# Graph convolution with a sparse adjacency: tiled rounds merged with full products, the row tiles' turns given by ScalarE, loads and stores both on SyncE

## The chip, the cores and the metric

The kernel runs on one NeuronCore of one Trainium2 chip. The metric is the device time of one execution in microseconds (us); lower is better. Times before are nine runs of the unchanged kernel. The profile is one further execution, taken by the hardware profiler.

## The reference

One layer: a symmetrised, rectified adjacency matrix is normalised by its degrees, applied to features, and the result goes through a rectifier, a residual sum and a layer norm.

```python
HW = jnp.einsum('bnf,fo->bno', H, W)              # H = x: (8, 4096, 256), W: (256, 256)
A_norm = jax.nn.relu((A + A.T) * 0.5)             # A = adj: (4096, 4096), sparse
D = jnp.sum(A_norm, axis=1)
DAD = d_inv_sqrt[:, None] * A_norm * d_inv_sqrt[None, :]
out = jnp.einsum('nm,bmo->bno', jnp.eye(N) - DAD, HW)
x = _layernorm(x + jax.nn.relu(out), axis=-1)     # eps 1e-5
```

Low-numbered nodes have many edges, high-numbered ones few. All arithmetic of the products is float32.

## The kernel before, in words

**First half (to about 593 us).** The adjacency is read in 512x512 blocks, symmetrised, and written to DRAM as `a_dram`; the features are multiplied by W, scaled, and written as `g_dram` (4096 rows of 2048 floats: 8 batches x 256). Row block 0 of the result is accumulated along the way. The change does not touch this half, save that line numbers move.

**Second half (from about 593 us).** The remaining 31 blocks of 128 result rows are worked off in 16 *units* (`SEQ`), two row blocks a unit, called b0 and b1. A block's result is 128 x 2048 floats, four PSUM banks of 128 x 512 (`py`, tags b0 and b1, four banks each: all eight banks). For each unit only those rows of `g_dram` that matter are fetched: lists made on VectorE (with a few small matmuls, `lists`) say which source rows have edges into the unit. GpSimd gathers 128 such rows at a time into one of twelve ring buffers `g` (1 MB) and the matching pieces of `a_dram` into `ga`, each with an indirect DMA. 268 such gathers are made. A slot is filled again when the oldest tile in the ring has been used up (`gather_ahead`, called once after every step). Two further sets of 128 rows, the hubs, stay in SBUF; only their adjacency rows `gh` are loaded per block.

**Steps.** `steps_of(u)` makes the order of a unit. There are two sorts of step.

- A *full step* is one tile (hub or ring) against one block: four products of 128x128 weights by 512 columns, one into each bank.
- A *tiled step* (a round) has up to eight operations, each with 64 source rows and 32 result rows, so that up to eight sit side by side in TensorE's array as tiles of 64x32. `tiled` runs the round in four *turns*; in turn m the operations on the upper 64 source rows write bank m, those on the lower 64 write bank m+2 (mod 4). Two row tiles must not write the same bank at one time, so each turn waits for the turn before the last: a `nop` on SyncE (a *tick*, line 1194) waits for the last matmul of the turn, and the first matmul of the turn after next waits for the tick.

Every float32 matmul stands twice in the trace, as two passes. A full product is two records of 128x512, a turn of eight operations is sixteen records.

Before, a full step and a round are always separate steps: 114 full steps and 112 rounds (838 operations), so 456 full products and 448 turns.

**Around the steps.** `run_later(2)` runs once after each step and counts down deferred work. When the last product of a block is in, `finish` queues four evictions on ScalarE (`evict`, line 760: PSUM to `y`, one buffer only, so the next block's eviction waits for VectorE's sum of the block before, line 770), and one step later the sum `z + y`, the statistics (779) and the normalisation (803) on VectorE; 14 counts (`LATE`) after that comes the store on SyncE's queue (813). When b0 of a unit is finished, `lists` puts 36 small matmuls on TensorE one step later, into two of the four b0 banks just evicted; VectorE reads them (236 to 241, 443 to 459) before it does the sum of b0. The next unit's first product for b0 into those banks waits for these reads. The residual rows `xr` (1 MB each) are loaded on ScalarE's DMA queue (`residuals`, line 754), 6 and 10 counts into a unit. All instructions of one engine run in the order in which they were recorded; `queue(...)` pins them there.

Of the kernel before, what the change touches and what calls it, by code (L numbers as in the profile page):

```python
# [25 lines left out]
HUBS = [*[2] * 15, 0]  # L26
# [41 lines left out]
def kernel(  # L68
# [25 lines left out]
    nc = tc.nc  # L94
    B, N, F = x.shape
    FO = w.shape[1]
    P = 128
# [9 lines left out]
    QU = P // E  # L107
# [1 line left out]
    HOLD = 10  # L109
    RING = 12  # L110
    REACH = 5
    LATE = 14
    EPS = 1e-5
    NK = len(KINDS)
    L = 64
    mid = KINDS.index(16), KINDS.index(51)
# [354 lines left out]
    with (  # L471
# [71 lines left out]
        held = {}  # L543
# [208 lines left out]
    def residual(i, engine):  # L752
        xr = blocks_pool.tile([P, B, F], F32, tag="adj", name=f"xr_{i}")
        engine.dma_start(xr, x[:, i * P : (i + 1) * P, :].rearrange("b p f -> p b f"))
        return xr
# [63 lines left out]
    def steps_of(u):  # L819

        kind_at = {}
        for k, kind in enumerate(KINDS):
            for s in range(FIRST[u][k], FIRST[u][k] + CAPS[u][k]):
                kind_at[s] = kind
        every = 255 if blocks(u) == 2 else 15
        whole = {0: [], 15: [], 240: []}
        todo = []
        for t in range(tiles[u]):
            pair = kind_at.get(2 * t), kind_at.get(2 * t + 1)
            if pair[0] == pair[1] and pair[0] in whole:  # L830
# [24 lines left out]
        def full(t, b):  # L855
            return [(t, None, b, None)]

        def weave(*several):
            several = [list(s) for s in several]
            total = [len(s) for s in several]  # L860
            out = []
            while any(several):
                at = max(range(len(several)), key=lambda k: (len(several[k]) / max(total[k], 1), total[k]))
                out.append(several[at].pop(0))
            return out

        held = range(HUBS[u])
        out = [full(-1, 0)] if HUBS[u] else []
        starts = [full(t, 0) for t in whole[15]]
        if not out and starts:  # L870
            out.append(starts.pop(0))
        out += weave(rounds[:first_b1], [full(-1 - h, 0) for h in held[1:]], starts)
        if blocks(u) == 1:
            return out + [full(t, 0) for t in whole[0]]
        out += [full(-1, 1)] if HUBS[u] else []
        rows = [[full(t, 0), full(t, 1)] for t in whole[0]]
        between = [[r] for r in rounds[first_b1 : max(last_b0 + 1, first_b1)]]
        out += chain.from_iterable(weave(between, rows))
        out += weave(
            [full(-1 - h, 1) for h in held[1:]],  # L880
            [full(t, 1) for t in whole[240]],
            rounds[max(last_b0 + 1, first_b1) :],
        )
        return out

    with (
        tc.tile_pool(name="ypool", bufs=2) as ypool,
# [32 lines left out]
        def queue(engine):  # L920

            traced = reversed(nc.cur_bb.bb.instructions)
            return tc.issue_after(next(i for i in traced if i.engine == engines[engine]))
# [154 lines left out]

        def residuals(rows):
            for i in rows:  # L1080
                with queue("act"):
                    xr[i] = residual(i, nc.scalar)


        ahead = {u: {k: SEQ[n + k] for k in (2, 3, 4) if n + k < NU} for n, u in enumerate(SEQ)}
# [59 lines left out]
        def follow(this, other):  # L1145
            tc.add_manual_dep(
                this.ins,
                other.ins.name,
                mybir.DependencyInfo(mybir.DependencyClass.Sync, mybir.DependencyReason.DATA),
                reason="two row tiles of the array take turns at a bank",  # L1150
            )
# [16 lines left out]
        NC = G // S  # L1168


        def tiled(u, step, last):

            for m in range(NC):
                ins = None
                for i in range(2):
                    c = (m + 2 * i) % NC
                    for op in step:
                        if op[1] != i:
                            continue
                        before = ins  # L1180
                        ins = product(
                            u,
                            op,
                            c,
                            slice(i * L, (i + 1) * L),
                            slice(op[3] * E, (op[3] + 1) * E),
                            False,
                            op in last and m >= NC // 2,
                        )
                        if before is None:  # L1190
                            if len(ticks) > 1:
                                follow(ins, ticks[-2])
                with queue("sp"):
                    ticks.append(nc.sync.nop())
                follow(ticks[-1], ins)

        for q, (u, step) in enumerate(steps):
            new = q == 0 or steps[q - 1][0] != u
# [14 lines left out]
            for b in touched:  # L1213
                if not py[2 * u + 1 + b]:
                    py[2 * u + 1 + b] = [
                        psum.tile([P, S], F32, tag=f"b{b}", name=f"py_{u}_{b}_{c}") for c in range(NC)
                    ]
            if step[0][1] is None:
                (op,) = step
                b = op[2]  # L1220
                hs = {(b, e) for e in range(QU)}
                assert not hs & begun or hs <= begun
                for h in hs:
                    left[h] -= 1
                for c in range(NC):
                    product(
                        u, op, c, slice(0, P), slice(0, P), not hs & begun, not any(left[h] for h in hs)
                    )
                begun |= hs
            else:  # L1230
                for op in step:
                    assert op[2:] in begun
                    left[op[2:]] -= 1
                last = [op for op in step if not left[op[2:]]]
                tiled(u, step, last)
            for op in step:
                t = op[0]
                uses_left[u, t] -= 1
                if t < 0:
                    load_hub_rows(SEQ[SEQ.index(u) + 1 :], -1 - t, op[2])  # L1240
            gather_ahead()
            run_later(2)
            for b in touched:
                if not any(left[b, e] for e in range(QU)):
                    if b == 0:
# [67 lines left out]
```

## Time and profile before

| | us |
|---|---|
| median of 9 runs (lowest to highest) | 1511.09 (1510.16 to 1513.78) |
| the profiled execution, own time | 1517.72 |
| its span, first to last instruction | 1515.5 |
| first and last start of a `py` matmul (the second half) | 592.6 and 1498.6 |
| PE, DVE, ACT, POOL busy over the span | 1393.5, 1039.9, 364.5, 770.4 |
| mean granted TensorE clock | 0.964 |
| DMA, whole run | 543.04 MB, 358 GB/s |

On the page, PE is matmul, PEld weight loads, DVE VectorE, ACT ScalarE, POOL GpSimd, SP SyncE; a q behind a name is the engine's sequencer. Matmul ends are modelled (a 512-column pass reads 589 ns although the next one may start 429 ns after it), so a busy PE is not a PE at its peak. For the second half the starts of matmuls tell more than the busy share. Line 1159 is the matmul of all products, 1194 the tick, 944 and 952 the gathers.

### The profile page before, as it was taken

How to read it: one execution, taken by the hardware profiler on the slowest of the kernel's cores; microseconds unless marked ns; L12 is line 12 of the kernel's file. 1: busy time of each engine (PE TensorE's matmuls, PEld its weight loads, DVE VectorE, ACT ScalarE, POOL GpSimd, SP SyncE). 2: the span in 40 equal slices, each digit the busy share in tenths (PEclk: the TensorE clock that was granted, in tenths of full speed). 3: DMA queues.
4: the chain of work that ended last, by engine and by line, in shares of the span. 5: the costliest groups of instructions: out<-in, count | busy, mean ns of one | idle time of the engine just before them, and what ended most of it. 6: DMA issues, size and time to landing. Idle time of an engine off the chain costs nothing.

```text
span 1515.5 us, 29693 instructions
## 1 busy us (share of the span) xinstructions
PE 1393.5 (92%) x11008; PEld 755.9 (50%) x11008; DVE 1039.9 (69%) x3173; ACT 364.5 (24%) x462; POOL 770.4 (51%) x1564
## 2 busy tenths in 40 slices
PE   6999998989999987999999999999999899998984
PEld 5877877767777753333433433333333343433331
DVE  5676578979956463208595897797408988899644
ACT  3555554544445450000001001001000110011111
POOL 3444010011313314764766667767745777786762
PEclk9999999989999999899999999999999999999996
DMA  9999999999989997998999999999977999999995
GB/s 357 368 361 400 394 378 362 354 338 352 350 316 348 336 397 283 368 398 321 391 367 371 357 391 383 384 373 373 398 268 264 381 354 406 386 372 402 380 378 173
DMA packets 217160, 543.04 MB, mean 358 GB/s; under 512 B 19370, under 2 KB 109194, under 8 KB 182426
## 3 DMA queue, kind: packets, MB, share of 16 engines
q0 software_dynamic: 55664, 283.87, 48.5%
q1 hardware_dynamic: 93472, 126.89, 24.5%
q10 hardware_dynamic: 67872, 130.32, 23.0%
q8 instruction: 89, 1.46, 0.4%
q14 instruction: 63, 0.51, 0.1%
HBM read 438.03 MB, written 136.34 MB: 379 GB/s over the span
## 4 chain that ended last, share of the span: by engine, by line
PE 47%; DMA 23%; DVE 19%; issue 5%; POOL 3%; ACT 2%; ACTq 0%; SPq 0%; POOLq 0%; DVEq 0%
PE py L1159 27%; DMA g<-g_dram,gi 10%; PE pg L607 9%; DMA ga<-a_dram,ai 6%; PE lead L565 5%; DVE sym L500 4%; DMA a_dram<-sym 3%; DVE sums L507 3%; PE tr L496 3%; PE xtr L596 3%; DMA xin<-in_x_dram 2%; DVE stats L779 2%; DVE xr L770 1%; DMA adj<-in_adj_dram 1%; POOL g L952 1%
## 5 line engine op out<-in xcount | busy, mean ns | idle before, releaser
L1159 PE MATMUL py<-g,ga 64*32 64x512 f32 (+1 forms) x7136 | 625.8, 615 | 35.8 <-DMA g<-g_dram,gi 30.4
L1159 PEld LDWEIGHTS py<-g,ga 64*32 64x32 f32 (+1 forms) x7136 | 230.1, 114 | 415.2 <-issue 342.8
L944 POOL DMA_INDIRECT ga<-a_dram,ai x268 | 289.7, 1081 | 136.2 <-PE py L1159 63.4
L952 POOL DMA_INDIRECT g<-g_dram,gi x268 | 300.2, 1120 | 110.5 <-issue 62.2
L760 ACT ACTIVATE y<-py,minus_r 128x512 f32<-128x512 f32 x120 | 75.9, 688 | 801.6 <-PE py L1159 622.4
L607 PE MATMUL pg<-w_sb,xt 128*128 128x256 f32 x1024 | 229.7, 382 | 5.8 <-ACT xt L597 4.0
L1159 PE MATMUL py<-g_hub,gh 128*128 128x512 f32 x480 | 222.2, 605 | 3.7 <-DVE pos_k L240 3.7
L500 DVE TENSOR_TENSOR sym<-tr,adj 128x512 f32<-128x512 f32 x256 | 161.8, 680 | 80.8 <-PE tr L496 79.2
L607 PEld LDWEIGHTS pg<-w_sb,xt 128*128 128x128 f32 x1024 | 194.1, 192 | 33.6 <-ACT xt L597 4.4
L508 POOL TENSOR_SCALAR uses<-sums 128x64 uint8<-128x64 f32 x64 | 27.6, 431 | 311.4 <-DVE sums L507 262.3
L507 DVE TENSOR_REDUCE sums<-sym 128x64 f32<-128x2048 f32 x64 | 145.3, 2276 | 52.2 <-ACT sym L504 52.2
L496 PE MATMUL tr<-ident,adj 128*128 128x128 f32 x1024 | 139.6, 287 | 28.2 <-DVE sym L500 16.0
L1159 PEld LDWEIGHTS py<-g_hub,gh 128*128 128x128 f32 x480 | 88.1, 191 | 132.4 <-issue 119.5
L504 ACT ACTIVATE sym<-sym 128x2048 f32<-128x2048 f32 x64 | 122.8, 1918 | 126.2 <-DVE sym L500 126.2
L443 DVE TENSOR_SCALAR low<-lists 128x17 f32<-128x17 f32 (+8 forms) x14 | 2.5, 175 | 213.7 <-PE lists L431 213.7
L496 PEld LDWEIGHTS tr<-ident,adj 128*128 128x128 f32 x1024 | 119.5, 147 | 55.1 <-DVE sym L500 33.5
L770 DVE TENSOR_TENSOR xr<-xr,y 128x2048 f32<-128x2048 f32 x31 | 70.8, 2285 | 50.9 <-ACT y L760 44.9
L596 PE MATMUL xtr<-ident,xin 128*128 128x128 f32 x512 | 74.1, 294 | 15.3 <-DVE sym L500 14.5
L803 DVE TENSOR_SCALAR xr<-xr,mv,root 128x256 f32<-128x256 f32 x248 | 84.6, 411 | 1.1
L779 DVE BATCH_NORM_STATS2 stats<-xr 128x6 f32<-128x256 f32 x248 | 84.1, 412 | 1.1
L565 PE MATMUL lead<-gt,strip 128*128 128x512 f32 x176 | 82.6, 593 | 0.0
L597 ACT COPY xt<-xtr 128x512 f32<-128x512 f32 x128 | 68.0, 592 | 45.9 <-PE xtr L596 36.9
(157 smaller groups left out, 1057.7 us busy)
## 6 DMA issues: line engine op xcount, KB each, us to landing
adj<-in_adj_dram SPq DMA_DIRECT2D x64, 1024.0 KB, 11.0
a_dram<-sym ACTq DMA_DIRECT2D x64, 1024.0 KB, 9.7
out_dram<-xr SPq DMA_DIRECT2D x31, 1024.0 KB, 20.3
xr<-in_x_dram ACTq DMA_DIRECT2D x28, 1024.0 KB, 20.6
xin<-in_x_dram SPq DMA_DIRECT2D x44, 512.0 KB, 11.7
g_dram<-gt ACTq DMA_DIRECT2D x22, 1024.0 KB, 7.6
xin<-in_x_dram POOLq DMA_DIRECT2D x20, 512.0 KB
g_dram<-held ACTq DMA_DIRECT2D x10, 1024.0 KB, 12.0
```

The lines of the kernel that those rows point to most:

```text
L496: ins = nc.tensor.transpose(pt[:, c * P : (c + 1) * P], tji[:, c, a * P : (a + 1) * P], ident)
L500: nc.vector.tensor_add(sym[:, a, :], pt, tij[:, a, :])
L504: nc.scalar.activation(sym, sym, AF.Relu, scale=0.5)
L507: nc.vector.tensor_reduce(sums, sym.rearrange("p a (c q) -> p a c q", q=E), AX.X, ALU.add)
L565: nc.tensor.matmul(lead[c], lhsT=strip, rhs=g[:, c * S : (c + 1) * S], start=not done, stop=len(done) == NB - 1, skip_group_check=True,)
L596: nc.tensor.transpose(pt[:, k, c, :], xin[b // H][:, b % H + k, c * P : (c + 1) * P], ident)
L607: ins = nc.tensor.matmul(pg[:, k * FO : (k + 1) * FO], lhsT=xt[:, b + k, c, :], rhs=w_sb[:, c, :], start=(c == 0), stop=(c == FC - 1),)
L770: nc.vector.tensor_add(z, z, y)
L779: nc.vector.bn_stats(stats[:, b, :], z[:, b, :])
L944: nc.gpsimd.indirect_dma_start(out=at if both else at[:, : E if one else P], out_offset=None, in_=a_pairs if both else a_groups if one els ...
L952: nc.gpsimd.indirect_dma_start(out=gt, out_offset=None, in_=g_dram, in_offset=bass.IndirectOffsetOnAxis(ap=gi[:, t : t + 1], axis=0), boun ...
L1159: return nc.tensor.matmul(py[2 * u + 1 + b][c][cols, :], lhsT=at[ps, off + cols.start : off + cols.stop], rhs=gt[ps, c * S : (c + 1) * S], ...
```

## The change

Rounds and full steps are merged. `beside` spreads the full steps of a stretch over its rounds; a round that gets one carries it as a ninth operation, and `tiled` puts one product of it behind every turn (bank m+1). The order within a unit is made anew: hub and early b0 products beside the rounds that touch only b0, everything in both blocks beside the middle rounds, and one full step (or the late rounds) at the end. Of 226 steps 157 are left: 45 full steps, 43 rounds without a full product, 69 rounds with one. Products and turns are the same in number (456 and 448). `run_later(2)` runs twice after a merged step.

The ticks move from SyncE to ScalarE (448 of them), the 28 residual loads from ScalarE's queue to SyncE's, where the stores are. `LATE` goes from 14 counts to 4.

```diff
-    LATE = 14
+    LATE = 4
...
+        def beside(several, fulls):
+
+            out, put = [], 0
+            for k, step in enumerate(several):
+                upto = len(fulls) * (k + 1) // len(several)
+                out.append(step + fulls[put] if put < upto else step)
+                out += fulls[put + 1 : upto]
+                put = max(upto, put)
+            return out + fulls[put:]
+
         held = range(HUBS[u])
-        out = [full(-1, 0)] if HUBS[u] else []
-        starts = [full(t, 0) for t in whole[15]]
-        if not out and starts:
-            out.append(starts.pop(0))
-        out += weave(rounds[:first_b1], [full(-1 - h, 0) for h in held[1:]], starts)
+        firsts = [full(-1 - h, 0) for h in held] + [full(t, 0) for t in whole[15]]
         if blocks(u) == 1:
-            return out + [full(t, 0) for t in whole[0]]
-        out += [full(-1, 1)] if HUBS[u] else []
-        rows = [[full(t, 0), full(t, 1)] for t in whole[0]]
-        between = [[r] for r in rounds[first_b1 : max(last_b0 + 1, first_b1)]]
-        out += chain.from_iterable(weave(between, rows))
-        out += weave(
-            [full(-1 - h, 1) for h in held[1:]],
-            [full(t, 1) for t in whole[240]],
-            rounds[max(last_b0 + 1, first_b1) :],
-        )
-        return out
+            return firsts[:1] + beside(rounds, firsts[1:]) + [full(t, 0) for t in whole[0]]
+        seconds = [full(-1 - h, 1) for h in held] + [full(t, 1) for t in whole[240]]
+        both = [full(t, b) for t in whole[0] for b in range(2)]
+        early, late = rounds[:first_b1], rounds[last_b0 + 1 :]
+        between = rounds[first_b1 : last_b0 + 1]
+        fills = firsts[1:] + both
+        ahead = min(len(firsts) - 1, len(early)) if between else len(firsts) - 1
+        kept = 0 if late else 1
+        mid = fills[ahead:] + (seconds[1 : len(seconds) - kept] if between else [])
+        rest = seconds[len(seconds) - kept :] if between else seconds[1:]
+        if late:
+            mid, rest = (fills[ahead:], seconds[1:])
+        return firsts[:1] + beside(early, fills[:ahead]) + seconds[:1] + beside(between, mid) + beside(late, rest)
...
         def residuals(rows):
             for i in rows:
-                with queue("act"):
-                    xr[i] = residual(i, nc.scalar)
+                with queue("sp"):
+                    xr[i] = residual(i, nc.sync)
...
-        def tiled(u, step, last):
+        def tiled(u, step, last, whole):
...
-                with queue("sp"):
-                    ticks.append(nc.sync.nop())
+                with queue("act"):
+                    ticks.append(nc.scalar.nop())
                 follow(ticks[-1], ins)
+                for op in whole:
+                    product(u, op, (m + 1) % NC, slice(0, P), slice(0, P), False, op in last)
...
+            alone = [op for op in step if op[1] is None]
+            if len(alone) == len(step):
...
             else:
...
+                assert all(hs <= begun for _, hs in spans)
+                tiled(u, [op for op in step if op[1] is not None], last, alone)
...
             gather_ahead()
-            run_later(2)
+            for _ in range(2 if 0 < len(alone) < len(step) else 1):
+                run_later(2)
```

The order at the end of a unit (F a full step, T8 a round of eight, T8F a round with a full product, 0 or 1 the block, ! where b0 is complete, * where b1 is). Unit 4 before: `F0 T8 F0 F0 F1 T6 F0 F1 T8 T8 T8 T8 T7! F1 F1*`; after: `F0 T8F0 F1 T6 T8F0 T8F0 T8 T8F1 T7F1! F1*`.

More of the change, by code (lines that the diff above doesn't have):

```diff
@@ L1217 @@
                     ]
[L1218 to L1222, printed above, removed]
+            spans = [(op, {tuple(op[2:])} if op[1] is not None else {(op[2], e) for e in range(QU)}) for op in step]
+            for _, hs in spans:
                 for h in hs:
                     left[h] -= 1
+            last = [op for op, hs in spans if not any(left[h] for h in hs)]
+            alone = [op for op in step if op[1] is None]
+            if len(alone) == len(step):
+                ((op, hs),) = spans
+                assert not hs & begun or hs <= begun
                 for c in range(NC):
-                    product(
-                        u, op, c, slice(0, P), slice(0, P), not hs & begun, not any(left[h] for h in hs)
-                    )
+                    product(u, op, c, slice(0, P), slice(0, P), not hs & begun, op in last)
                 begun |= hs
             else:
[L1231 to L1235, printed above, removed]
+                assert all(hs <= begun for _, hs in spans)
+                tiled(u, [op for op in step if op[1] is not None], last, alone)
             for op in step:
```

## The prediction

> **What bounds the kernel now.** Only the second half changes. It runs from 592.6 to 1498.6 us (906.0 us); before it and behind it the work is the same. I read the stretches first: busy time, granted clock, DMA share and rate.
>
> ```profile
> core 0: us, PE busy (x) PEld busy (x) DVE busy (x) ACT busy (x) POOL busy (x), PEclk, DMA share, GB/s
> 592.60:627.04 34.44, 24.09 (x130) 7.42 (x128) 19.92 (x61) 0.70 (x2) 27.14 (x26) 0.80 0.95 349
> ...
> 700.00:800.00 100.00, 100.00 (x908) 38.61 (x914) 76.57 (x287) 4.84 (x8) 69.39 (x65) 1.00 0.99 364
> ...
> 1100.00:1200.00 100.00, 95.47 (x1012) 35.65 (x1010) 56.41 (x213) 10.01 (x16) 60.05 (x60) 0.97 0.81 293
> ...
> 1300.00:1400.00 100.00, 90.22 (x920) 37.12 (x919) 92.50 (x345) 10.02 (x16) 76.69 (x72) 0.95 1.02 388
> ```
>
> TensorE is busy all through 700 to 800 at full clock: there nothing but its own pace counts. Later DMA is close behind (share 1.02 at 388 GB/s), and a gather comes late now and then. The waits say how much, over the second half (us in total, times, longest):
>
> ```profile
> ACT y L760 <- DVE xr L770: 151.6, 14, 14.9
> ...
> PEld py L1159 <- SPq L1194: 58.5, 203, 1.8
> ...
> PE py L1159 <- DMA g<-g_dram,gi: 30.4, 14, 5.8
> ...
> PE lists L294 <- DVE kind L284: 6.8, 2, 4.5
> ...
> PE lists L431 <- DVE val L426: 5.8, 1, 5.8
> ...
> PE py L1159 <- DVE pos_k L240: 3.7, 3, 1.9
> ...
> PE py L1159 <- SPq L1194: 1.5, 2, 0.9
> ```
>
> The trap is the second line. 58.5 us of waits on ticks belong to weight loads, which run ahead of the matmuls; matmuls themselves waited 1.5 us. So there is next to nothing to win from slack for the ticks. What switching between full products and rounds costs is in the timeline of TensorE:
>
> ```profile
> 815.05 1.96 PE L1159 MATMUL py<-g_hub,gh 128*128 128x512 f32 x4
> 818.86 1.98 PE L1159 MATMUL py<-g_hub,gh 128*128 128x512 f32 x4 [1.85 <-DVE pos_k L240]
> 820.78 3.66 PE L1159 MATMUL py<-g,ga 64*32 64x512 f32 x64
> 824.37 3.70 PE L1159 MATMUL py<-g_hub,gh 128*128 128x512 f32 x8
> 827.91 3.60 PE L1159 MATMUL py<-g,ga 128*128 128x512 f32 x8
> 831.34 3.60 PE L1159 MATMUL py<-g_hub,gh 128*128 128x512 f32 x8
> 834.87 5.56 PE L1159 MATMUL py<-g,ga 64*32 64x512 f32 x52
> ```
>
> Four full products after four full products start 3.43 us apart (827.91 to 831.34), 0.858 each. Out of a round it is 3.59 (820.78 to 824.37), the first full step after a round takes 3.54, the last before a round 3.53. Taking the starts of all matmuls of the second half in that view: a turn or product is followed after 0.858 us by one of its own sort; a turn by a full product after 0.995 (+0.137, 52 cases); a full product that follows a turn takes 0.962 (+0.104, all 52); a turn follows a full product after 0.952 (+0.094). One excursion out of the rounds and back costs 0.335 us.
>
> The 906.0 us add up so: 456 products + 448 turns = 904 x 0.858 = 775.6; 52 excursions x 0.335 = 17.4; 14 sets of list matmuls x 1.33 = 18.7; three waits for list reads x 1.95 = 5.9 (815.05 to 818.86 is 3.81 where two products take 1.8 to 1.9). The other 88 us are late data and slow clock: 17 before 627 us (34.4 minus 17.8 of work), 71 later. In the 71: about 23 of the 30.4 on gathers, 13.6 on late lists, some 25 from half clock (51 us of it after 627, at most half lost), ticks and late weight loads.
>
> **The change part by part.**
>
> *Merged steps.* In the program's order the change from turn to full product occurs 276 times (52 before) and back 277 times (53): a product stands behind each of four turns in 69 steps. 224 more excursions x 0.335 = **+75.0 us**, all on TensorE, which nothing covers. No row shows an excursion of one single product. Bounds: 0, if the product's weight load and the emptying of the array hide behind the neighbours; 0.37, the sum of the rounded lines above. I take 0.335, since the 0.962 is the same for hub products, whose data landed long before, as for freshly gathered ones: it is no wait for data.
>
> The Trainium skill, TensorEngine Tiling, Key Properties, speaks against the change as well: changing the tiling mode, not just the tile, drains TensorE. Its page TensorE: Matmul & The Clock Gate (Part 2, step 4) puts the drain at about 128 cycles, 53 ns at 2.4 GHz; two drains an excursion would make an estimated 24 us in place of 75. The rows show three times that, and they decide.
>
> *End of a unit.* Twelve units leave list matmuls whose banks the next unit's first product needs. Before, nine of them had another step in between. Now all end on one step, the lists, and then the next unit's first product. VectorE needs 3.4 us (pos_k L240) from the last list matmul; the two products to free banks cover only 1.7:
>
> ```profile
> 753.45 0.62 DVE L240 TENSOR_TENSOR pos_k<-incl_k,lists 128x448 f32<-128x448 f32 x1
> ...
> 754.64 2.28 DVE L770 TENSOR_TENSOR xr<-xr,y 128x2048 f32<-128x2048 f32 x1
> ...
> 757.02 0.69 ACT L760 ACTIVATE y<-py,minus_r 128x512 f32<-128x512 f32 x1 [9.63 <-DVE xr L770]
> ```
>
> (The list matmuls of this boundary end at 750.66.) 9 x 1.95 = **+17.6**.
>
> *Ticks on ScalarE.* Behind the tick now stand evictions on the same queue, and b1's eviction waits for VectorE's sum of b0 (the last line above). Queued behind it are the next unit's ticks. It ends 8.8 us after the lists (757.02 plus four activations, 2.4). The third turn of the next unit is the first to need one of them: at 3.6 + 2 x 0.86 for the held products, then turn, product, turn, product (4.1), at 9.4. Covered, with 0.5 to spare; the cover is the wait just priced and the products between turns. Units 6 and 8 start with a bare round, whose third turn is due at 7.1: 2 x 2.0 = **+4**. Elsewhere a tick costs what it did on SyncE (a 17 ns record).
>
> *Loads and stores on SyncE.* 28 loads move past 31 stores. A load can now stand behind a store that waits for VectorE (L803), and only L770 waits for the load, tens of us later; issuing takes 0.4 to 0.8 us on either queue. 0; if the cover fails, 2 us at L770 once a unit, and then only through the eviction of b1. Shorter `LATE` brings stores forward, in front of nothing that TensorE waits for: 0.
>
> *Gathers.* The same 268. POOL's queue issues them after 157 steps in place of 226, and merged steps hold tiles longer: with 0.858 a product and 0.335 an excursion, the mean life of a tile goes from 6.2 to 9.6 us, and 34 tiles (11 before) have under 16 us from free slot to first use. That speaks for more late gathers. Against it TensorE needs them more slowly: the half's 328 MB (362 GB/s over 906 us) over some 965 us are 340 GB/s, against 384 to 388 where DMA was tight. Of the 71 us all or none may go (0 to -71); I take half, **-36**, as the two pull against each other.
>
> Sum: 75.0 + 17.6 + 4 - 36 = +60.6. On the profiled execution's 1517.7 that is 1578.3; it lay 6.6 over the median of 1511.1, so **1571.7** for the median.
>
> **The rivals.**
>
> 1. *The excursion is free inside a step* (ends faster). The product behind a turn has no landing to wait for, its weights could be there early. 4 + 17.6 - 36 = -14: 1497. The point from which it decides: (36 - 21.6) / 224, under 0.064 us an excursion the kernel is no slower. Against: 52 of 52 at 0.962. Chance 0.09.
> 2. *Feeding gets no better.* Short leads once a unit cost what the slower pace wins: relief 0, +97: 1608. For: the 34 short leads; against: 340 GB/s. Chance 0.15.
> 3. *ScalarE holds the ticks.* If the sum of b0 comes 2 us later than at 754.64, twelve unit starts lose 1.5 us: +18: 1590. For: 14.9 us as the longest wait; against: the sum ended 6.1 to 6.7 us after the lists at every such boundary of the timeline. Chance 0.10.
> 4. *The clock drops.* Emptied arrays might be taken for idleness. 69 merged steps last some 8 us; a tenth of that at half clock is +28: 1600, all of it far more. Against: full clock from 700 to 800 with switches. Chance 0.04.
>
> **How the numbers follow.** The forecast has 0.62. Its own range is relief 71 to 0: 1537 to 1608. Rivals 2 and 3 lie in it; 1 lies out, and 4 in part, with the upper edge of 2. Range 1535 to 1606. A change under 0.2% (3 us) can't be told from none. Faster 0.09 (rival 1), same 0.02, slower 0.89.
>
> **What would show it.** In the profile after: in a merged step products and turns alternate some 2.05 us a pair (1.72 if rival 1 holds); waits of `py` for pos_k around 12 times, about 1.9 us each; tick waits by matmuls near 4 us; waits on gathers under 30; clock 0.96 or better; the second half 950 to 980 us. Pairs near 1.72 would make the prediction wrong outright; waits on gathers over 60 or tick waits over 20 would move it up.

## The result and the profile after

The changed kernel takes 1634.4 us (median of ten runs, 1620.96 to 1640.33) where the kernel before takes 1511.09: a ratio of 1.080, with a 95% interval of 1.078 to 1.082. The forecast was 1571.7, with a range up to 1606. The direction was right, the size was not: 123 us slower instead of 61.

The profiled execution took 1629.16 us, 5.2 under the median of its kernel; that of before lay 6.6 over its own. So some 12 of the 123 us are in no comparison of the two profiles.

The changed kernel's page, its span, granted clock and DMA queues:

```profile
span 1627.4 us, 29632 instructions
...
PEclk9999999999999888999999999999999998999995
...
q0 software_dynamic: 55664, 284.04, 45.4%
q1 hardware_dynamic: 122592, 156.25, 29.0%
q10 hardware_dynamic: 38752, 100.96, 15.8%
```

The queues are new in one respect. SyncE's (q1) now carries the residual loads too: 122592 packets instead of 93472, 156 MB instead of 127, and ScalarE's (q10) carries that much less.

The stretches of the changed kernel, busy time of each engine, clock, DMA share and rate:

```profile
core 0: us, PE busy (x) PEld busy (x) DVE busy (x) ACT busy (x) POOL busy (x), PEclk, DMA share, GB/s
...
700.00:800.00 100.00, 98.17 (x807) 27.70 (x808) 68.63 (x264) 7.27 (x12) 55.91 (x54) 1.00 0.81 291
1100.00:1200.00 100.00, 95.78 (x753) 23.99 (x751) 44.82 (x170) 2.73 (x5) 51.78 (x50) 0.98 0.75 276
1300.00:1400.00 100.00, 83.77 (x825) 30.11 (x826) 76.94 (x289) 9.69 (x16) 62.63 (x59) 0.93 0.91 348
```

From 700 to 800 us TensorE is as busy as before and at full clock. The counts of passes don't compare, as a turn has up to sixteen and a product two; counted in the program's order, 98 turns and products start there where 112 did. Most of that is switching: the stretch has 36 excursions instead of 7, and 29 of them take 10 of the 12 us that 14 turns or products last. From 1300 to 1400 it is another matter (84 turns and products instead of 96): TensorE is idle for 16 us and the clock falls to 0.93. The waits of the second half tell on what (us in total, times, longest):

```profile
DVE xr L770 <- DMA xr<-in_x_dram: 35.3, 2, 22.7
PE py L1167 <- DMA g<-g_dram,gi: 34.9, 14, 5.3
...
PE py L1167 <- DVE pos_k L240: 17.9, 11, 1.9
...
PE lists L294 <- DVE kind L284: 13.8, 1, 13.8
PE py L1167 <- ACTq L1202: 12.5, 2, 9.0
```

Waits for `pos_k` came as forecast. The first line had no counterpart before: VectorE's sum (L770) waits for residual rows. Three shorter waits of the sum (16.5 us) stand under "issue" in the same view, but each ends within 0.1 us of the landing of the rows that it needs. TensorE's waits for `kind` and for two ticks follow from these. TensorE's timeline shows both sorts of loss, the switching (a turn of sixteen records, then two records of a product) and one of the long waits:

```profile
1327.71 1.98 PE L1167 MATMUL py<-g_hub,gh 128*128 128x512 f32 x4 [1.67 <-DVE pos_k L240]
1329.63 1.09 PE L1167 MATMUL py<-g,ga 64*32 64x512 f32 x16
1330.65 1.13 PE L1167 MATMUL py<-g_hub,gh 128*128 128x512 f32 x2
1331.70 1.09 PE L1167 MATMUL py<-g,ga 64*32 64x512 f32 x16
1332.72 1.13 PE L1167 MATMUL py<-g_hub,gh 128*128 128x512 f32 x2
...
1384.10 0.55 PE L294 MATMUL lists<-kind,ones 128*128 128x448 bf16 x1 [13.78 <-DVE kind L284]
```

A turn and a product take 2.07 us (1329.63 to 1331.70) where two of one sort take 1.72. Where the 13.78 us begin is seen on SyncE's DMA queue and on VectorE, in the same kernel:

```profile
1298.46 0.37 SPq L813 DMA_DIRECT2D out_dram<-xr  x1
1298.93 13.48 SPq L754 DMA_DIRECT2D xr<-in_x_dram  x1
1339.23 0.37 SPq L813 DMA_DIRECT2D out_dram<-xr  x1
1339.70 7.67 SPq L754 DMA_DIRECT2D xr<-in_x_dram  x1
```

```profile
1351.71 2.29 DVE L770 TENSOR_TENSOR xr<-xr,y 128x2048 f32<-128x2048 f32 x1 [12.51 <-DMA xr<-in_x_dram]
```

At 1298.46 a store goes out, and the load recorded behind it follows at once. Issuing it takes 13.48 us in place of half a microsecond, and its rows are there 52.8 us later, at 1351.71, after VectorE has waited 12.51. From 1298 to 1352 SyncE's queue moved 3.4 MB and the gathers' queue 17.4 MB, by the sizes of their packets in the trace. The Trainium skill, DMA: Bandwidth & Descriptors, section Queues, rings and completion order, has each DMA engine take its queues in turn, a packet at a time. The trace agrees as far as it goes: from 1308 to 1312 us the gathers' queue and SyncE's had 249 and 154 packets, but mostly of 8 KB and of 1 KB, so 1.47 and 0.15 MB. With the loads on ScalarE's queue (e8, below) SyncE's and ScalarE's moved 0.23 and 0.19 MB in the same four microseconds, beside 1.23 of the gathers.

**Where the time went.** The second half lasts 1010.4 us (591.7 to 1602.1) instead of 906.0, and the tail behind the last `py` matmul 25.3 instead of 16.9. I take the second half apart as the prediction did: 775.6 for products and turns, 18.7 for list matmuls, excursions at their price, 1.95 us for each unit end with a wait for `pos_k`; what is left is late data and slow clock. The starts of all matmuls give the excursion of the changed kernel: 1.019 from a turn of eight to its product (0.995 before), 0.962 for the product behind a turn as before, 1.056 from a product back to a turn, which holds that 0.104 and 0.094. So it costs 0.161 + 0.104 + 0.094 = 0.359. The 0.024 more is no new cost: before, too, the first turn of eight behind a product is followed by the next turn after 0.883 and not 0.858 (31 cases), a step that the prediction's three don't hold, so there an excursion costs 0.36 as well. In what follows the 52 of before stay at the prediction's price. The 276 excursions make 99.1 us in place of 17.4. Twelve unit ends make 23.4 in place of 5.9 (the waits for `pos_k` themselves are 17.9 in place of 3.7). What is left is 93.6 where it was 88.4: the 36 us of relief did not come.

### The profile page after: what moved, and what is told of

Same layout as the page of the kernel before. It is cut to its first block, busy times and chain, and to the rows that moved or that the text cites. A ratio compares the mean times of both kernels' runs of the same rounds, so it can differ in the third digit from the quotient of the medians.

```text
span 1627.4 us, 29632 instructions
## 1 busy us (share of the span) xinstructions
PE 1466.2 (90%) x11008; PEld 698.3 (43%) x11008; DVE 1038.6 (64%) x3173; ACT 361.0 (22%) x462; POOL 768.6 (47%) x1564
## 3 DMA queue, kind: packets, MB, share of 16 engines
q1 hardware_dynamic: 122592, 156.25, 29.0%
## 4 chain that ended last, share of the span: by engine, by line
PE 46%; DMA 25%; DVE 17%; issue 7%; POOL 4%; ACT 1%; SPq 0%; ACTq 0%; POOLq 0%; DVEq 0%
PE py L1167 28%; DMA g<-g_dram,gi 9%; PE pg L607 8%; DMA xr<-in_x_dram 6%; PE lead L565 5%; DVE sym L500 3%; DMA a_dram<-sym 3%; DMA xin<-in_x_dram 3%; PE tr L496 3%; DVE sums L507 2%; PE xtr L596 2%; DMA ga<-a_dram,ai 2%; POOL ga L952 2%; DVE stats L779 2%; DVE xr L803 1%
## 5 line engine op out<-in xcount | busy, mean ns | idle before, releaser
L1167 PE MATMUL py<-g,ga 64*32 64x512 f32 (+1 forms) x7136 | 683.4, 611 | 50.5 <-DMA g<-g_dram,gi 34.9
L1167 PEld LDWEIGHTS py<-g,ga 64*32 64x32 f32 (+1 forms) x7136 | 182.2, 112 | 534.0 <-issue 459.7
L952 POOL DMA_INDIRECT ga<-a_dram,ai x268 | 297.8, 1111 | 120.9 <-issue 54.8
L960 POOL DMA_INDIRECT g<-g_dram,gi x268 | 289.8, 1081 | 124.8 <-issue 65.2
L1167 PE MATMUL py<-g_hub,gh 128*128 128x512 f32 x480 | 248.2, 635 | 17.9 <-DVE pos_k L240 17.9
L1167 PEld LDWEIGHTS py<-g_hub,gh 128*128 128x128 f32 x480 | 82.4, 193 | 172.3 <-issue 141.5
L770 DVE TENSOR_TENSOR xr<-xr,y 128x2048 f32<-128x2048 f32 x31 | 70.8, 2284 | 81.3 <-DMA xr<-in_x_dram 35.3
L940 POOL DMA_DIRECT2D gh<-a_dram x60 | 35.2, 589 | 119.6 <-PE py L1167 118.2
L803 DVE TENSOR_SCALAR xr<-xr,mv,root 128x256 f32<-128x256 f32 x248 | 83.8, 409 | 1.1
```

What stands on the lines that cost most here:

```text
L803: nc.vector.tensor_scalar(z[:, b, :], z[:, b, :], mv[:, b, 0:1], rstd[:, b : b + 1], ALU.subtract, ALU.mult,)
L952: nc.gpsimd.indirect_dma_start(out=at if both else at[:, : E if one else P], out_offset=None, in_=a_pairs if both else a_groups if one els ...
L960: nc.gpsimd.indirect_dma_start(out=gt, out_offset=None, in_=g_dram, in_offset=bass.IndirectOffsetOnAxis(ap=gi[:, t : t + 1], axis=0), boun ...
L1167: return nc.tensor.matmul(py[2 * u + 1 + b][c][cols, :], lhsT=at[ps, off + cols.start : off + cols.stop], rhs=gt[ps, c * S : (c + 1) * S], ...
```

## The experiments

Ten experiments (e5 to e8, e13 to e18) ran on chips where the kernel before takes 1512 to 1514 us, about as in the first profiles. The other eight (e1 to e4, e9 to e12) ran on chips where it takes 1759 and 1763; their numbers are compared only with each other, by ratio, and they have a part of their own at the end.

The second half of each kernel, taken apart as above (us):

| kernel | second half | excursions | unit ends | left: late data, slow clock | half clock |
|---|---|---|---|---|---|
| before | 906.0 | 17.4 | 5.9 | 88.4 | 64.9 |
| changed | 1010.4 | 99.1 | 23.4 | 93.6 | 78.5 |
| changed, once more (e5) | 1007.0 | 99.1 | 23.4 | 90.2 | 78.5 |
| two steps kept (e6) | 991.3 | 86.2 | 5.9 | 104.9 | 88.7 |
| two products behind every second turn (e7) | 973.3 | 49.5 | 23.4 | 106.1 | 78.5 |
| loads on ScalarE (e8) | 996.2 | 99.1 | 23.4 | 79.4 | 54.6 |
| products last (e13) | 953.0 | 24.8 | 23.4 | 110.5 | 88.7 |
| LATE 14 (e16) | 974.9 | 99.1 | 23.4 | 58.1 | 41.0 |
| three parts undone (e14) | 919.9 | 21.5 | 5.9 | 98.2 | 68.3 |
| four parts undone (e17) | 920.4 | 21.5 | 5.9 | 98.7 | 51.2 |
| before, hubs first (e15) | 906.2 | 10.7 | 5.9 | 95.3 | 54.6 |
| before, LATE 4 (e18) | 970.2 | 17.4 | 5.9 | 152.6 | 122.4 |

Excursions are at 0.335 in the two old orders of before and e15 and in e18, at 0.359 elsewhere; at 0.36 before would have 1.3 us more there and 1.3 less left. The last column is the time at half clock by the clock's records; what it costs is part of what is left, at most half of it. A profile is one execution: that of before lay 6.6 us over its median, that of the changed kernel 5.2 under.

### The yardstick (e5)

The changed kernel, unedited.

> The changed kernel itself, unedited, as the yardstick of this call. On a chip like that of the first profiles 1.080 times the kernel before (about 1634 us beside 1511). On a chip like that of the first four experiments, where the kernel before took 1759 us, the loads' queue is worth at most 10 us, so it should stand within 0.01 of the kernel with the loads on ScalarE there (1.066).

1628.3 us, ratio 1.077 (1.074 to 1.081): within 6 us of the first measurement.

### The price of an excursion (e7, e13)

```diff
-                for op in whole:
-                    product(u, op, (m + 1) % NC, slice(0, P), slice(0, P), False, op in last)
+                for op in whole if m % 2 else ():
+                    for c in ((m + 1) % NC, (m + 2) % NC):
+                        product(u, op, c, slice(0, P), slice(0, P), False, op in last)
```

> Two products behind every second turn instead of one behind each; the same steps, products and turns, 138 excursions in place of 276. Theory (TensorE pays per excursion): 138 x 0.359 = 49.5 us less than the changed kernel, 0.033 of the ratio, half to two thirds of what putting all four products behind all four turns saves. Rival (the time is lost to the steps being merged at all: fewer steps, fewer calls that fetch, longer lives of the tiles): under 15 us.

e13 puts all four products behind the fourth turn:

```diff
-                for op in whole:
-                    product(u, op, (m + 1) % NC, slice(0, P), slice(0, P), False, op in last)
+            for op in whole:
+                for c in range(NC):
+                    product(u, op, c, slice(0, P), slice(0, P), False, op in last)
```

> Products of a merged step behind all four turns: 69 excursions in place of 276. On a chip like the first: theory (0.359 us an excursion, all exposed) 74 us less than the changed kernel's 1628 to 1634, so 1554 to 1560 or 1.030; rival (part is given back as late lists and late loads, since the order that feeds them stays the same and TensorE comes sooner): 55 to 65 us less, 1.037 to 1.043.

e7: 1586.4 us (ratio 1.047, 1.042 to 1.051), 42 less than e5. e13: 1576.2 (1.044, 1.041 to 1.047), 52 to 58 less than the changed kernel's two medians. e13 falls clearly short of 74. The 42 of e7 can't be told from 49.5, as its runs lie between 1576 and 1597 us. The waits of TensorE in e13 say where the rest went:

```profile
PE py L1167 <- DMA g<-g_dram,gi: 33.3, 14, 5.5
PE lists L294 <- DVE kind L284: 23.8, 1, 23.8
PE py L1167 <- DVE pos_k L240: 17.6, 11, 1.8
PE py L1167 <- ACTq L1202: 15.6, 2, 9.6
```

The one wait for `kind` is 6.6 us in e5 (13.8 in the first profile of the same kernel), 20.5 in e7 and 23.8 in e13: where TensorE is quicker, it waits longer for the lists behind the late residual rows. Without that wait the second halves are 1000.4, 952.8 and 929.2 for 276, 138 and 69 excursions: 0.345 and 0.342 us for each one saved, beside 0.36 by the starts. So the excursion is paid nearly in full inside a merged step, and the rival that part of the price is given back holds as well.

### The end of a unit (e6)

```diff
-        kept = 0 if late else 1
+        kept = 0 if late else min(2, len(seconds) - 1)
```

> Two full steps instead of one stand behind the last merged step of nine units (1, 2, 4, 5, 6, 7, 9, 13, 14). Theory (excursions and the wait at the unit's end, each at its measured price): 36 fewer excursions (240 changes from turn to full product in place of 276) x 0.359 = -12.9 us, and waits for pos_k fall from 11 to 3, -13: about 26 us less than the changed kernel on the same chip, 0.017 of the ratio. Rival (the wait at the unit's end only stands where a late gather or list would stand anyway): 13 us or less.

1612.1 us (1.060, 1.055 to 1.066). That is 16 less than e5 by the medians and 25 by the ratios; the runs lie between 1598 and 1622, too far apart to tell 16 from 26. In the profiles the second half is 15.7 shorter. The waits for `pos_k` fell as expected, from 17.5 to 5.9 us; 36 excursions fewer are 12.9. But the wait for `kind` went from 6.6 to 12.9, gathers from 34.3 to 38.0, and half clock from 78.5 to 88.7: what is left grew by 14.7.

### The queues and LATE (e8, e16, e18)

The residual loads back on ScalarE's queue:

```diff
-                with queue("sp"):
-                    xr[i] = residual(i, nc.sync)
+                with queue("act"):
+                    xr[i] = residual(i, nc.scalar)
```

> The changed kernel with the residual loads back on ScalarE's queue. Theory (two late residual loads on the queue shared with the stores cost VectorE 35 us and through it lists, half clock and tail some 40 us): on a chip like that of the first profiles 25 to 45 us less than the changed kernel. Rival (the late loads stand where TensorE has slack, or the loads come late on the other queue as well): within 10 us of it. In the prediction's terms: the load's queue was put at 0.

1613.2 us (1.067, 1.063 to 1.070), 15 less than e5: between the two. VectorE's long waits for residual rows are gone (one of 4.4 us is left, near the end), no issue takes over 2 us, the tail is 19.2. TensorE's waits:

```profile
PE py L1167 <- DMA g<-g_dram,gi: 42.6, 24, 6.1
...
PE lists L294 <- DVE kind L284: 1.1, 1, 1.1
```

The waits for lists and ticks are gone, but gathers come late 24 times in place of 14. Now LATE alone, with the loads still on SyncE:

```diff
-    LATE = 4
+    LATE = 14
```

> The changed kernel with LATE 14 instead of 4, nothing else: a store is issued ten counts later, loads and stores still share SyncE's queue. Theory (the load is late because the queue is shared and gathers take the DMA engines with 8 KB packets against 1 KB): within 8 us of the changed kernel, VectorE still waiting for residual loads at the sum. Rival (it is the store in front of it, issued sooner): 10 to 20 us less, like the loads on ScalarE's queue.

1598.3 us (1.057, 1.054 to 1.060): 30 to 36 us less than the changed kernel's medians, twice what the queue gave. My theory fell; the rival's sign was right, but not its size. The waits of e16:

```profile
PE py L1167 <- DMA g<-g_dram,gi: 31.5, 14, 7.2
...
PE lists L294 <- DVE kind L284: 1.2, 1, 1.2
PE py L1167 <- ACTq L1202: 0.9, 1, 0.9
```

Its stretch from 1300 to 1400 us:

```profile
1300.00:1400.00 100.00, 93.78 (x1019) 34.11 (x1004) 88.60 (x331) 9.69 (x16) 74.03 (x68) 1.00 1.01 377
```

97 turns and products start in it where the changed kernel had 84, at full clock. Between the two profiles the second half differs by 35.5 us: the waits for `kind` and for ticks fall by 24.2 together, those on gathers by 3.4, and 37.5 us less pass at half clock. And SyncE's DMA queue of e16:

```profile
1307.11 18.16 SPq L754 DMA_DIRECT2D xr<-in_x_dram  x2
1335.03 11.62 SPq L813 DMA_DIRECT2D out_dram<-xr  x2
```

(A line with x2 holds two issues and the time between them.) Loads go out in pairs ahead of the stores, as no store that waits for VectorE stands in front of them. From issue of a load to the sum that uses it there are 95 us in the median, against 51.5 in the changed kernel and 53.1 before (counted over 28 loads). Issues still take up to 13 us on the full queue, but now it is stores that are slow, and TensorE waits for none. One sum, near the end, still waits 22.8 us for its rows; TensorE loses 0.9 by it.

Loads on ScalarE's queue (e8) take away the same waits for `kind` and ticks but give back only half as much, because waits on gathers grow to 42.6 us there and are 31.5 in e16. Why gathers are less late with LATE 14 on the shared queue wasn't told apart.

LATE 4 alone, in the kernel before, was to show whether LATE costs without the shared queue:

```diff
-    LATE = 14
+    LATE = 4
```

> The kernel before with LATE 4, nothing else; loads stay on ScalarE's queue. Theory: within 0.2% of the kernel before. Rival (sooner stores cost in any order): 5 to 12 us slower, 1.003 to 1.008, in waits on gathers.

1580.8 us (1.045, 1.042 to 1.048): 68 us slower, far beyond both theories. Its waits, and one case of them on TensorE and on SyncE's DMA queue:

```profile
PE py L1159 <- SPq L1194: 88.9, 17, 6.9
PE py L1159 <- DMA g<-g_dram,gi: 8.0, 4, 5.2
```

```profile
690.31 1.94 PE L1159 MATMUL py<-g,ga 64*32 64x512 f32 x28
698.67 3.66 PE L1159 MATMUL py<-g,ga 64*32 64x512 f32 x28 [6.42 <-SPq L1194]
```

```profile
698.18 0.38 SPq L813 DMA_DIRECT2D out_dram<-xr  x1
```

The store waits for VectorE's normalisation (its last eight, L803, start at 695.48 and take 2.67). Before, the ticks are on SyncE, so at LATE 4 the ticks of the next unit are queued behind that store: it goes out at 698.18, the tick follows, and the third turn starts at 698.67 after 6.42 us. Seventeen such waits make 88.9 us, and the time at half clock nearly doubles. So the move of the ticks to ScalarE is what LATE 4 needs, and the loads on SyncE are what LATE 4 then holds up in the ticks' stead.

### All priced parts undone (e14, e17)

Products last, two steps kept, loads on ScalarE (the edits of e13, e6 and e8 together).

> Products behind all four turns, two steps kept at the unit's end, residual loads on ScalarE's queue; merged steps, LATE 4 and ticks on ScalarE stay. Theory (the three parts are all that cost, and the feeding is as before): 1.002 to 1.010 of the kernel before on a chip like the first. Rival A (merging itself costs, by fewer calls that fetch and ticks behind evictions): 1.015 or more. Rival B (the feeding does get better once TensorE is not slowed, the prediction's relief): under 1.000.

1533.5 us (1.013, 1.011 to 1.016): between the theory and rival A. e17 has LATE 14 besides.

> Three parts undone (products behind all four turns, two steps kept, loads on ScalarE's queue) and LATE 14 as well; merged steps and ticks on ScalarE stay. Theory (LATE 4 hurts only through the queue shared with the loads): as with LATE 4, 1.010 to 1.016 of the kernel before, with some 40 us or more of waits on gathers. Rival (stores issued sooner run beside a unit's first gathers): 1.000 to 1.007, waits on gathers back near 30 us.

1533.9 us (1.013, 1.010 to 1.016), the same. So in this order LATE costs nothing where loads and stores have a queue each and ticks are on ScalarE. The waits of e17:

```profile
PE py L1167 <- DMA g<-g_dram,gi: 46.8, 26, 5.2
PE py L1167 <- DVE pos_k L240: 7.1, 4, 1.8
```

What stays of the change is 1.3%, and the row that grew is the gathers': 46.8 us in 26 waits against 30.4 in 14. The merged order feeds worse at the old pace. Which of its traits does that, the fewer calls that fetch or the longer lives of tiles, wasn't told apart.

### Fewer excursions in the old order (e15, e9)

```diff
-        out += weave(rounds[:first_b1], [full(-1 - h, 0) for h in held[1:]], starts)
+        early = rounds[:first_b1]
         if blocks(u) == 1:
+            out += weave(early, [full(-1 - h, 0) for h in held[1:]], starts)
             return out + [full(t, 0) for t in whole[0]]
+        out += weave([full(-1 - h, 0) for h in held[1:]], starts)
         out += [full(-1, 1)] if HUBS[u] else []
+        out += early
```

> The kernel before with the early rounds behind the hub steps: 32 excursions in place of 52. On a chip like the first: theory 20 x 0.335 = -6.7 us, ratio 0.9955; rival (leads under 16 us for 36 tiles in place of 11 give it back as late gathers; on the slower chip it came out at 1.026): 1.000 or more, with more than 40 us of waits on gathers in place of 30.

1519.9 us: 1.005 (1.003 to 1.008) of the kernel before, slower. The 6.7 us of excursions were saved, and what is left grew by 6.9 (88.4 to 95.3) between the two profiles. By the medians it grew by more: the times differ by 8 us though the second halves are alike, as before's profiled execution was slow for its kernel and e15's was not. The waits of e15 on gathers are fewer us but more times than before; the 40 us expected did not show there:

```profile
PE py L1162 <- DMA g<-g_dram,gi: 28.6, 19, 3.4
...
PE lists L431 <- DVE val L426: 4.9, 1, 4.9
```

Beyond its products and turns each of the units 1 to 4, 6, 7, 0 and 8 takes 0.4 to 4.9 us less than before; unit 5 takes 5.0 more and units 9 to 13 together 11.2 more. That the shorter leads of the tiles do this is argued from the leads, not shown by one row. e9 was the same kernel on a chip of the other kind:

> The kernel before, with the rounds that touch only b0 moved behind the hub steps of both blocks, so that the full steps at a unit's start stand together: 32 excursions in place of 52, nothing else changed. Theory (an excursion costs 0.335 us wherever it stands): 20 x 0.335 = -6.7 us, ratio 0.9955. Rival (what is saved is given back, since the first row tiles of 14 units must land after 10.3 us of full steps as before but the slots they free come later: 36 tiles in place of 11 have under 16 us from free slot to first use): within 0.2% of the kernel before, or slower.

1.026 (1.023 to 1.029) there.

### On the two other chips (e1 to e4, e10 to e12)

| | edit | ratio to before on its chip |
|---|---|---|
| e1 | changed, loads on ScalarE | 1.066 (1.062 to 1.071) |
| e4 | changed order, queues and LATE of before | 1.061 (1.058 to 1.064) |
| e2 | changed, products last | 1.036 (1.033 to 1.039) |
| e10 | the same | 1.030 (1.027 to 1.033) |
| e11 | three parts undone | 1.013 (1.010 to 1.016) |
| e3 | order of before, queues and LATE of the change | 1.005 (1.003 to 1.008) |
| e12 | before, loads alone on SyncE | 1.003 (1.000 to 1.005) |

> The changed kernel with one thing undone: the residual loads are on ScalarE's DMA queue again. Theory (loads and stores on one queue of 1 KB packets get through at half the rate while 8 KB gathers compete; VectorE then waits for a residual, and TensorE behind it): the waits of VectorE for residuals (35.3 us in 2 waits) and the wait of the lists for VectorE (13.8) go, some 25 to 45 us less, 1590 to 1610 us. Rival (the loads are late because they are recorded late): no change, 1625 to 1640. Second rival (loads on ScalarE hold the ticks): over 1640.

> The changed kernel, its order of steps and its queues, but in a merged step the four products of the full tile stand behind all four turns, not one behind each turn. Theory (an excursion out of the turns and back costs 0.36 us, and there are 207 fewer of them): 207 x 0.359 = 74 us less, 1560 us (1545 to 1575). Rival (the order within units and the feeding of tiles cost the time, not the switching): 1620 to 1640.

> The order of steps and the separate full steps of before, but the ticks on ScalarE, the residual loads on SyncE and stores 4 counts after. Theory: without merged steps the switching (82 us) and the unit ends (17.5 us) go; what is left over the kernel before is the price of the moved queues, 5 to 40 us: 1515 to 1550 us. Rival (the moved ticks are the cost, since they stand behind evictions): over 1570.

> The merged steps and the order of the changed kernel, with the queues of before: ticks on SyncE, residual loads on ScalarE, stores after 14 counts. Theory: switching 82 + unit ends 17.5 stay, the late residuals go: 1595 to 1615 us. If the queues cost nothing: 1630 or more. If the queues are most of it: under 1560.

> The changed kernel with the four products of a merged step behind all four turns: 69 excursions in place of 276, same steps. Theory: 207 x 0.359 = 74 us less than the changed kernel, ratio 1.028 to the kernel before; with the 42 us of half as many excursions (138) that makes three points on one line. Rival (the price is per product that changes weights, or part of it is hidden): 55 us or less, ratio 1.041 or more. The prediction's relief of 36 us would show if nothing but excursions stood between: then the ratio would be nearer 1.01.

> The changed kernel with three parts undone together: products behind all four turns, two full steps kept at the unit's end, residual loads on ScalarE's queue. 60 excursions beside 52 before (+3 us); waits for pos_k as before. What remains of the change: merged steps (so fewer calls that fetch tiles), ticks on ScalarE, LATE 4. Theory (the three parts are all that cost): 1.002 to 1.010 of the kernel before. Rival (the merged steps cost by themselves, through late data or ticks behind evictions): 1.015 or more. The prediction's relief, were it there, would make it faster than before: 0.98.

> The kernel before with nothing changed but the residual loads' queue: on SyncE, with the stores, LATE 14. Theory (one queue for loads and stores delays a load behind stores in all orders): 5 to 15 us slower, ratio 1.003 to 1.010, with VectorE waiting for a residual load at the sum. Rival (the delay needs the changed order, where a store is issued 10 counts sooner and the next load stands right behind it): within 0.2%.

The absolute numbers expected of e1 to e4 were meant for the first chip and can't be held against these. By ratio the order of merit is much the same: the merged order is what costs (e3 against e1 and e4), and the products between the turns are about half of it, as far as e2 and e1 compare, which differ in the loads' queue too. e11 agrees with e14. e12 shows that loads behind stores are harmless in the old order at LATE 14 (at the edge of what can be told). e3 shows that all three edits of queues and LATE together cost 0.5% in the old order; on a chip like the first that wasn't run. What the changed kernel itself takes on such a chip was not measured.

TensorE's timeline of e3 shows how these chips differ:

```profile
762.33 1.09 PE L1159 MATMUL py<-g,ga 64*32 64x512 f32 x16 [0.70 <-ACTq L1194]
767.42 1.96 PE L1159 MATMUL py<-g,ga 64*32 64x512 f32 x16 [4.00 <-ACTq L1194]
773.86 5.29 PE L1159 MATMUL py<-g,ga 64*32 64x512 f32 x64 [4.48 <-issue]
```

Turns stop for 4 to 5 us in front of a tick that nothing visible holds. The tick does nothing but wait for the turn's last matmul. With the ticks paired to the turns in order, in the first profile of before a tick comes 0.70 us after the start of its turn's last matmul in the median, over 1.5 us after it in 7 of 446 cases, and 2.3 at most; in e3 0.77 in the median, but over 1.5 in 136 of 446, and up to 12.5 (a late tick also holds up the one behind it). It is as late on SyncE (e12: 131 cases, 0.85) as on ScalarE. The half clock goes along with it (256 us in the second half of e3). What delays the signal of the matmul is open.

## Why the prediction was right or wrong

**Merged steps: right.** The excursion is 0.36 and not 0.335, since a turn right behind a product takes 0.024 longer, before as after; the upper bound of 0.37 was the nearer figure. In the account that makes 81.7 us for +75.0. e7 and e13 show that nearly all of it is exposed; rival 1 (free inside a step) is out. The pair took 2.07 where 2.05 was to show.

**End of a unit: right.** Waits for `pos_k` in 11 places of 1.9 us at most, 14.2 us more than before for +17.6; e6 takes the waits away for seven of them.

**Ticks: right place in a unit, wrong units and cause.** Units 6 and 8, with 2.0 each, had no such wait. Units 14 and 15 had one each, of 3.5 and 9.0 us, at the third turn as forecast. The long one:

```profile
1588.49 2.29 DVE L770 TENSOR_TENSOR xr<-xr,y 128x2048 f32<-128x2048 f32 x1 [5.70 <-issue]
```

```profile
1590.88 2.42 ACT L760 ACTIVATE y<-py,minus_r 128x512 f32<-128x512 f32 x4 [14.19 <-DVE xr L770]
```

```profile
1591.06 11.59 PE L1167 MATMUL py<-g,ga 64*32 64x512 f32 x128 [8.96 <-ACTq L1202]
```

The rows for that sum landed at 1588.41; the eviction waits for the sum, and the tick stands behind the eviction. This is the way of rival 3 (ScalarE holds the ticks behind a late sum), but at two unit starts and not at twelve, and for late rows. With LATE 14 ticks cost 0.9.

**Loads and stores, and LATE: the step that failed.** Both were put at 0, the one because "only L770 waits for the load, tens of us later", the other because stores come "in front of nothing that TensorE waits for". The text itself saw that "a load can now stand behind a store that waits for VectorE", but priced each edit by itself. At LATE 4 store and load are issued as a pair, and 2 MB go through one queue in the time that 1 MB had; with gathers on the same DMA engines that took 52.8 us, more than the cover. Behind L770 on VectorE stands the making of the next lists, for which TensorE waits, and then the clock falls. In place of the 0, LATE 14 gives back 30 to 36 us (e16) and the loads' own queue 15 (e8). In the kernel before, LATE 4 costs 68 us by another way (e18). Of the cases run on chips like the first, LATE 4 is a 0 where neither ticks nor loads stand behind the stores (e14 against e17).

**Gathers, -36: the size came near with LATE 14, the mechanism did not show.** With LATE 14 what is left falls from 88.4 to 58.1, -30 between the profiles and some 22 by the medians. But waits on gathers are 31.5 us where they were 30.4, and 42.6 in e8 at the same slow pace; under 30 was forecast. What fell is waits for lists (13.6 to 1.2) and the time at half clock (64.9 to 41.0). Waits for lists are as short in e14 and e17 at the old pace, so a slower TensorE isn't what shortened them: that part of the size is luck. A slower pace does seem to help, as more is left at the old pace with the same queues (98 in e14, 79 in e8). With LATE 4 on the shared queue the late residual rows took all of it back (93.6). So rival 2 (feeding gets no better) gave a time nearer to the measured one, 1608, but its mechanism, the short leads, is not what decided here; late gathers show in e17 and e8 and, less surely, in e15. How much of e16's relief is owed to the loads' long lead wasn't told apart.

**Clock: rival 4 out.** 0.961 for the mean clock, as forecast; half clock follows waits and falls to 41 us with LATE 14 though the excursions stay.

**The sum.** The second half was put at 906.0 + 60.6 = 966.6. e16, the change without its LATE, measures 974.9. For the changed kernel, 1634.4 - 1571.7 = 62.7 is made, to within 0.4, of: second half 43.8 (35.5 from LATE, by e5's profile 32.1; 6.7 from the excursion's price; the rest small), tail 8.4, and 11.8 from where the two profiled executions lie about their medians, less 0.9 at the start. The tail was in no term. In the merged order on chips like the first it is 25.3 in all profiles with loads on SyncE and 19.2 with loads on ScalarE; that the last unit's sums come late for their rows, and statistics queue up behind them, fits this but wasn't tested.

No kernel here beats the one before.

## What to carry to other kernels

Price the edits of one queue together, not one by one: list for each queue what now stands in front of what, and what each entry waits for. A transfer that was issued 50 us ahead on its own queue is late with the same lead behind another megabyte, once indirect gathers keep the DMA engines busy. And where an engine is fed just in time, time saved on it can come back as late data (e13, e15); measure what is left besides the price of the edit, and look at the row that was to shrink, not only at the sum.

## What the runs showed of the hardware

- Full products between tiled turns cost 0.36 us for each change there and back by the starts of matmuls, the same in the old order and in merged steps; bunching them saved 0.34 each.
- A DMA issue of 1 MB on a queue that still holds a megabyte took up to 17.4 us on SyncE instead of 0.5, and what is behind it on that queue waits as long.
- On two of the chips the signal that a tiled turn is done came up to 12 or 13 us after the start of its last matmul (2.3 at most in the first profile of before), and the same kernel took 16% longer. A comparison across chips needs the kernel before on each of them.
